# Stores of copied sums on ScalarE's queue, value copies on VectorE, fewer and larger transfers, and a guard between two finishing chunks

## The chip, the cores and the metric

The kernel runs on one core of a Trainium2 chip. The metric is device time in microseconds (us) of one execution; a kernel's time is the median of several runs. Engines are named as the profile names them: PE is TensorE (PEld its weight loads), DVE is VectorE, ACT is ScalarE, POOL is GpSimd and SP is SyncE. SPq, ACTq and so on are the instruction sequencers of these engines, where transfers (DMAs) are issued and where an engine waits for others. L1270 is line 1270 of the kernel before.

## The reference, cut to what matters

The input is x, 4 images of 128 channels and 64 x 64 positions, in float32. Layer 0 is a group norm, a deformable 3 x 3 convolution (offsets and masks from two small convolutions, four-corner bilinear samples) and a residual. Layer 1 takes the 4096 positions of an image as tokens and does attention with 16 heads of 8 values, a small feed-forward part, and a mixture of 8 experts, two per token:

```
x = x + deform_conv(group_norm(x))
t = to_tokens(x)
heads = layer_norm(t).reshape(B, S, 16, 8)
q = quantum_ring(heads + rx_theta)          # cosines and their running products
ctx = softmax(q @ q.T / sqrt(8)) @ q        # queries, keys and values are all q
x1 = layer_norm(ln_t + ctx @ w_comb.T + b_comb)
h = relu((cos(x1[:8]) * cos(ry)) @ w1.T + b1)
t = t + layer_norm(x1 + h @ w2.T + b2)
t = t + top2_experts(layer_norm(t))
```

Queries, keys and values are the same array q. The exponentials of the scores are most of the work: 4 images x 16 heads x 4096 x 4096, less what the symmetry of q @ q.T saves.

## The kernel before, in words

An image ("batch" b, 0 to 3) is cut into 8 chunks of 512 tokens (ch, or sc for a chunk of queries) and the 16 heads into 4 groups (g) of 4.

The main loop (from L1417) goes over **runs**. A run is one group and one chunk of queries against a list of key tiles t of 128 keys. For each key tile, one **step**, `scores` does 4 score matmuls on PE (L1261) and two exponentials of 128 x 1024 on ACT (L1270), and `context` sums with 4 matmuls on PE into one PSUM bank `acc` (L1281). A step takes two exponentials of 1.08 us each by their issue on ACT, some 1.86 us. Because the score matrix is symmetric, some runs give their exponentials transposed to another run (`turn`, L1140, on DVE, through DRAM), which multiplies them in `from_turned` (L1214).

Batch 0 has no earlier batch to hide its preparation behind. Its first runs use the chunks as they come, so their sums are partial. The first 26 runs (`run < opening`, `by_act` in the code) copy `acc` to an SBUF tile `cu` on ACT (L1491). `park_sums` has SP store `cu` to a DRAM tile `partd` (L1126), and the next run on the same group and chunk loads it back (L1456) and PE adds it into `acc` with the identity as weights. There are two `cu` tiles. From run 26 on DVE does the copies (L1493, L1495), and their stores stay on SP.

**Preparation** (`prepare`) of a batch is a generator. `deform` gathers corners from a DRAM table on POOL (L625), weighs and sums them on DVE (L645, L650, L651), transposes and parks them through DRAM (`smd`, L698 and L731). `convolved` does the convolution on PE for a chunk and ends in `features`: layer norm, cosines and products on DVE (to L822), then

* POOL copies the products q8 into the value tile `fx`, spaced by the column of ones (L823), and SP stores it to `fqd` in 4 transfers, one for each group (L827);
* PE transposes q8, DVE makes a high and a low part `hiT` and `loT` (L838, L839), and SP stores each twice into the keys `kTd` and twice into the queries `qTd` (L846, L847): 8 transfers of 256 KB.

`load_keys` and `load_queries` fetch them on SP (L1239, L1241, L1249).

**Finishing** (`finish`) of a chunk comes after the fourth group's context is parked: loads, `attention_out`, then `feed_forward` and `experts`, and a store of the result (L1081). Up to two finishing generators are alive at once, each taking the next chunk from the list `done`.

The order of all of this on PE, DVE, SP and POOL is written by a planner, the class `Beside`, while the program is built. In each step (`step`) it adds preparation, finishing and multiplications of turned exponentials beside the attention. A piece with PE work ("fill" below) is taken at most once a step after run 12, from a credit of 0.44 us a step, by rank: turned work first, finishing with ranks 1 and 2, preparation with 0.5 or 2. Work that must wait for something is put into a list by its planned time (`later`) and emitted when that time has come (`flush`). The planner only plans: on the chip every engine takes its own queue in order. After the last attention step, `drain` emits what is left, one job after the other. The exponentials on ACT are not ordered by hand.

The functions that the diff touches:

Of the kernel before, what the change touches and what calls it, by code (L numbers as in the profile page):

```python
# [22 lines left out]
P = 128  # L23
# [5 lines left out]
CH = 512  # L29
# [3 lines left out]
HD = 8  # L33
NGRP = 4
# [20 lines left out]
QG = 4 * QW  # L55
QL = QG
# [146 lines left out]
def need(pe=0.0, dve=0.0, lat=0.0, hold=False, after=0.0):  # L203

    return pe, dve, lat, hold, after


def ve(n, ops=1):  # L210

    return ops * (0.17 + n / 960.0)
# [6 lines left out]
def tr(n):  # L219

    return 0.13 + 0.115 * n
# [3 lines left out]
def kernel(  # L225
# [22 lines left out]
    nc = tc.nc  # L248
# [12 lines left out]
    beside = Beside()  # L261
# [11 lines left out]
    def misc(name):  # L273
        if alone:
            return ps_s.tile([P, 2, 512], F32, tag="sc", name=name)[:, 0, :]
        return ps_m.tile([P, 512], F32, tag="misc", name=name)
# [141 lines left out]
    for i in range(NFX):  # L418
        t = big.tile([P, 4, QR], F32, name=f"fx{i}")
        nc.gpsimd.memset(t, 0.0)  # L420
        h = t[:, :, : HEADS * QW].rearrange("p j (h d) -> p j h d", d=QW)
# [3 lines left out]
    def parked(shape, name, n=2):  # L425
        return [
            [dram.tile(shape, F32, name=f"{name}{i}_{c}") for c in range(NCH)] for i in range(n)
        ]

    x2d = parked([P, 4, C], "x2d", NB)  # L430
    fqd = parked([NGRP, P, 4, QL], "fqd")
    kTd = parked([P * NGRP, CH], "kTd")
    qTd = parked([P * NGRP, CH], "qTd")
# [3 lines left out]
    partd = [[dram.tile([P, CH], F32, name=f"part{g}_{c}") for c in range(NCH)] for g in range(NGRP)]  # L437
# [355 lines left out]
    def features(b, ch, x2, mean, rstd):  # L793

        yield from layer_norm_stats(x2, mean, rstd, "lt")

        def temp(name, shape=(P, 4 * C), dt=F32):
            return work.tile(list(shape), dt, tag="p2", name=f"{name}{b}_{ch}", bufs=NP2)

        fx, f4 = fxs[ch % NFX]  # L800
        xt, a, n, r = temp("xt"), temp("ra"), temp("rn"), temp("rr")
        yield need(dve=ve(128, 4))
        normalized(xt.rearrange("p (i c) -> p i c", c=C), x2, mean, rstd)
        beside.later(
            beside.dve,
            lambda: nc.sync.dma_start(out=xtd[b][ch].rearrange("p i c -> p (i c)"), in_=xt),
        )
        yield need(dve=ve(512, 2))
        a8 = a.rearrange("p (h d) -> p h d", d=HD)
        x8 = xt.rearrange("p (h d) -> p h d", d=HD)  # L810
        nc.vector.tensor_tensor(a8, x8, rx_sb[:, None, :].to_broadcast([P, 64, HD]), ALU.add)
        yield from cosine(a, a, n, r, ve(512))
        c8 = a.rearrange("p (j h d) -> p j h d", j=4, d=HD)
        q8 = n.rearrange("p (j h d) -> p j h d", j=4, d=HD)
        yield need(dve=ve(64, 7))
        nc.vector.tensor_tensor(q8[:, :, :, 0], c8[:, :, :, 1], c8[:, :, :, 2], ALU.mult)
        for d in range(3, HD):
            nc.vector.tensor_tensor(q8[:, :, :, 0], q8[:, :, :, 0], c8[:, :, :, d], ALU.mult)
        yield need(dve=ve(64, 7), lat=0.2)
        nc.vector.tensor_tensor(q8[:, :, :, 1], c8[:, :, :, 0], c8[:, :, :, 1], ALU.mult)  # L820
        for d in range(2, HD):
            nc.vector.tensor_tensor(q8[:, :, :, d], q8[:, :, :, d - 1], c8[:, :, :, d], ALU.mult)  # L822
        beside.later(beside.dve, lambda: nc.gpsimd.tensor_copy(f4[:, :, :, :HD], q8))  # L823

        def put_values():
            for g in range(NGRP):
                nc.sync.dma_start(out=fqd[b % 2][ch][g], in_=fx[:, :, QG * g : QG * g + QL])  # L827

        beside.later(beside.dve + 2.0, put_values)

        yield need(pe=tr(4), dve=ve(512, 2))
        pt = misc(f"fT_ps{b}_{ch}")
        for i in range(4):
            nc.tensor.transpose(pt[:, P * i : P * (i + 1)], n[:, P * i : P * (i + 1)], ident)
        hi, lo = temp("hiT"), temp("loT")
        nc.vector.tensor_copy(hi.bitcast(F32R), pt)  # L838
        nc.vector.tensor_tensor(lo.bitcast(F32R), pt, hi, ALU.subtract)  # L839

        def put(part, fT):

            kd = kTd[b % 2][ch].rearrange("(h l r d) n -> l r h d n", l=2, r=2, d=HD)
            qd = qTd[b % 2][ch].rearrange("(h r l d) n -> l r h d n", l=2, r=2, d=HD)
            for rep in range(2):
                nc.sync.dma_start(out=kd[part, rep], in_=fT)  # L846
                nc.sync.dma_start(out=qd[part, rep], in_=fT)  # L847

        beside.later(beside.dve - ve(512), lambda: put(0, hi))
        beside.later(beside.dve, lambda: put(1, lo))  # L850
        prepared[b, ch] = beside.dve + 9.0
        featuring.pop(0)

# [41 lines left out]
    def attention_out(b, ch, r, aT, a4):  # L895


        yield need(dve=ve(512))
        nc.vector.tensor_tensor(r, r, bc4(b_comb), ALU.add)
        yield need(dve=ve(512), lat=0.2)  # L900
        nc.vector.tensor_tensor(aT, aT, a4.rearrange("p i c -> p (i c)"), ALU.mult)
        for i in range(4):
            if i % 2 == 0:
                yield need(pe=2 * MM128, dve=ve(512) if i else 0.0, lat=0.0 if i else FREE, hold=not i)
            if i == 0:
                po = misc(f"ao_ps{b}_{ch}")
            by_columns(
                po[:, C * i : C * (i + 1)], aT[:, P * i : P * (i + 1)], wcomb_sb, True, True
            )
        nc.vector.tensor_tensor(r, r, po.rearrange("p (i c) -> p i c", c=C), ALU.add)  # L910
        m = work.tile([P, 4], F32, tag="ln_m", name=f"m1{b}_{ch}")
        rs = work.tile([P, 4], F32, tag="ln_r", name=f"r1{b}_{ch}")
        yield from layer_norm_stats(r, m, rs, "ln")
        yield need(dve=ve(128, 4))
        normalized(a4, r, m, rs)
        yield need(dve=ve(512, 2), lat=0.2)
        nc.vector.tensor_tensor(a4, a4, bc4(g1), ALU.mult)
        nc.vector.tensor_tensor(a4, a4, bc4(beta1), ALU.add)
# [165 lines left out]
    def finish(b, ch):  # L1084
        x4 = temp2(f"x4_{b}_{ch}")
        nc.sync.dma_start(out=x4, in_=x2d[b][ch])

        rows = atd[b][ch].rearrange("g (h d) n -> (g h) d n", d=32)
        aT = temp2(f"aT{b}_{ch}", (P, CH))
        nc.sync.dma_start(out=aT, in_=rows[:, :HD])  # L1090
        rd = work.tile([P, CH // HD], F32, tag="rd", name=f"rd{b}_{ch}")
        nc.sync.dma_start(out=rd, in_=rows[:, HD].rearrange("h (q n) -> h q n", q=HD))
        r = temp2(f"r{b}_{ch}")
        nc.sync.dma_start(out=r, in_=xtd[b][ch])
        yield need(lat=4.0)
        yield need(dve=0.6, lat=0.1)
        nc.vector.reciprocal(rd, rd)
        yield need(lat=3.5)
        nc.sync.dma_start(out=rdd[b][ch].rearrange("h q n -> (h q) n"), in_=rd)
        yield need(lat=6.0)  # L1100
        a4 = temp2(f"a4_{b}_{ch}")
        nc.sync.dma_start(
            out=a4.rearrange("p i c -> p (i c)"),
            in_=rdd[b][ch].rearrange("h q n -> h (q n)")[:, None, :].to_broadcast([HEADS, HD, CH]),
        )
        yield from attention_out(b, ch, r, aT, a4)
        yield from feed_forward(b, ch, x4, a4)
        yield from experts(b, ch, x4)


    def park_context(b, g, sc, cu):
# [8 lines left out]

        beside.later(beside.dve, put)

    def park_sums(g, sc, cu, when):

        def put():
            nc.sync.dma_start(out=partd[g][sc], in_=cu)  # L1126
            storing.discard((g, sc))

        storing.add((g, sc))
        beside.later(when, put)  # L1130

# [90 lines left out]

    landing = {}
    fetched = {}
    groups, done, active = {}, [], []

    def finishing():

# [125 lines left out]
    for n, (run, t) in enumerate(steps):  # L1356
        b, g, sc = runs[run][:3]
# [50 lines left out]
    n = issued = begun = 0  # L1408
    beside.rate = 1.0
    with tc.manual_schedule(engines={PE, DVE, SP, POOL}):  # L1410
# [6 lines left out]
        while n < len(steps):  # L1417
# [10 lines left out]
            run, t = steps[n]  # L1428
            b, g, sc, ts, kind = runs[run]
# [21 lines left out]
            if t == ts[0]:  # L1451
                if kind in (MORE, LAST):
                    if (g, sc) in storing:
                        beside.flush()
                    cu = work.tile([P, 512], F32, tag="cu", name=f"cu{run}", bufs=NCU)
# [23 lines left out]
            by_act = run < opening  # L1479
# [8 lines left out]
            if kind in (WHOLE, FIRST):  # L1488
                cu = work.tile([P, 512], F32, tag="cu", name=f"cu{run}", bufs=NCU)
            if by_act:  # L1490
                nc.scalar.copy(cu, acc)  # L1491
            elif kind in (WHOLE, FIRST):
                nc.vector.tensor_copy(cu, acc)  # L1493
            else:
                nc.vector.tensor_tensor(cu, cu, acc, ALU.add)  # L1495
            if kind in (WHOLE, LAST):
                park_context(b, g, sc, cu)
            else:
                park_sums(g, sc, cu, beside.now + 3.0 if by_act else beside.dve)
        alone.append(True)  # L1500
        beside.drain()

# [72 lines left out]
```

## Time and profile before

| | us |
|---|---|
| median of 11 runs | 7601.65 |
| lowest and highest | 7593.96 and 7617.57 |
| the profiled execution | 7605.18 |
| span of its profile, from the first to the last instruction | 7603.2 |

| engine | busy us | share of the span |
|---|---|---|
| PE | 7126.1 | 94% |
| ACT | 6865.0 | 90% |
| DVE | 4465.9 | 59% |
| PEld | 2378.2 | 31% |
| POOL | 1661.8 | 22% |

The DMA engines moved 1689.51 MB in 909788 packets. Busy shares are means over stages with different limits: the first 900 us, in which batch 0 is prepared, and the last 83 us, in which nothing but finishing is left, look different from the middle. The idle time in front of an instruction is put down to what released it.

### The profile page before, as it was taken

The numbers are of one execution on the slowest core, as the hardware profiler recorded it, in microseconds if no ns is written. First come the engines' busy times: TensorE is split into PE (matmuls) and PEld (weight loads), VectorE is DVE, ScalarE is ACT, GpSimd is POOL, SyncE is SP. The second block draws the span as 40 slices with busy tenths as digits, with TensorE's granted clock in tenths as the row PEclk, the third lists the DMA queues.
The fourth block names the chain that finished last, engine by engine and source line by source line (L and its number), as shares of the span: only waits on it lengthen the run. The fifth ranks groups of instructions, "written<-read, shape, count | busy, mean of one in ns | idle before, by whom it ended". The sixth has DMA issues, their size and how long they took to land.

```text
span 7603.2 us, 180754 instructions
## 1 busy us (share of the span) xinstructions
PE 7126.1 (94%) x73848; PEld 2378.2 (31%) x73848; DVE 4465.9 (59%) x8950; ACT 6865.0 (90%) x7467; POOL 1661.8 (22%) x1326
## 2 busy tenths in 40 slices
PE   3689999899999999999999999989999999999997
PEld 2122222223333333333333323323333333333333
DVE  6756356667444867776554677766444544555534
ACT  0578999889999999999999988989999999999995
POOL 5544034443000432422000334431000000000000
PEclk6799999999999999999999999999999999999998
DMA  5677567978445878887645688897454466666661
GB/s 178 210 214 222 139 220 239 296 230 294 149 170 196 294 232 270 279 279 240 210 177 183 232 280 296 284 316 248 174 182 161 142 232 232 233 221 243 222 204 64
DMA packets 909788, 1689.51 MB, mean 222 GB/s; under 512 B 150754, under 2 KB 384124, under 8 KB 858268
## 3 DMA queue, kind: packets, MB, share of 16 engines
q1 hardware_dynamic: 809102, 1371.37, 54.4%
q0 software_dynamic: 92160, 302.06, 12.1%
q8 instruction: 579, 9.49, 0.5%
q10 hardware_dynamic: 7694, 4.52, 0.2%
q14 instruction: 253, 2.07, 0.1%
HBM read 1027.51 MB, written 650.14 MB: 221 GB/s over the span
## 4 chain that ended last, share of the span: by engine, by line
PE 83%; DMA 7%; DVE 4%; issue 2%; ACT 2%; SPq 1%; POOL 1%; another core or an unknown queue 1%; ACTq 0%; POOLq 0%; DVEq 0%
PE acc L1281 40%; PE sc L1261 25%; PE acc L1214 5%; PE e_ps L281 4%; PE conv_ps L281 4%; DMA et<-etd 3%; PE f_ps L281 2%; ACT e L1270 2%; DMA sT<-smd 1%; PE om_ps L533 1%; DVE v L645 1%; DMA etd<-st 1%; POOL v L625 1%; DMA cu<-part 0%
## 5 line engine op out<-in xcount | busy, mean ns | idle before, releaser
L1270 ACT ACTIVATE e<-sc 128x1024 f32<-128x1024 f32 x7400 | 6850.7, 1079 | 553.3 <-PE sc L1261 369.7
L1281 PE MATMUL acc<-e,qf 128*9 128x512 f32 (+1 forms) x29600 | 3942.5, 601 | 28.1 <-ACT cu L1491 10.4
L1261 PE MATMUL sc<-qT,kT 32*128 32x512 f32 x14800 | 2373.4, 499 | 167.1 <-ACT e L1270 92.6
L1261 PEld LDWEIGHTS sc<-qT,kT 32*128 32x128 f32 x14800 | 945.1, 183 | 3629.5 <-ACT e L1270 3109.1
L625 POOL DMA_INDIRECT v<-tab,idx x1152 | 1458.8, 1266 | 1589.4 <-DVE tr L686 961.7
L1140 DVE STREAM_TRANSPOSE st<-e 128x1024 f32<-128x1024 f32 x792 | 937.3, 1222 | 763.3 <-ACT e L1270 663.0
L1281 PEld LDWEIGHTS acc<-e,qf 128*9 128x9 f32 (+1 forms) x29600 | 682.5, 91 | 623.9 <-issue 352.1
L396 POOL TENSOR_TENSOR r<-ln_t,expo 128x4 f32<-128x4 f32 x96 | 112.2, 1169 | 3107.2 <-DVE ln_t L394 3059.9
L645 DVE TENSOR_TENSOR v<-v,wt 128x1536 f32<-128x1536 f32 x384 | 667.0, 1737 | 113.5 <-DMA v<-tab,idx 88.7
L1214 PE MATMUL acc<-et,qv 128*9 128x128 f32 x12672 | 508.9, 277 | 59.1 <-DMA et<-etd 49.0
L1065 DVE TENSOR_TENSOR eo<-e_ps,gt 128x512 f32<-128x512 f32 x256 | 175.2, 686 | 557.1 <-PE e_ps L281 550.5
L650 DVE TENSOR_TENSOR v<-v 128x768 f32<-128x768 f32 x384 | 367.2, 956 | 10.1
L281 PE MATMUL conv_ps<-sT,wconv_sb 128*32 128x256 f32 x4320 | 350.5, 398 | 9.3 <-DMA sT<-smd 7.0
L1214 PEld LDWEIGHTS acc<-et,qv 128*9 128x9 f32 x12672 | 270.2, 90 | 262.8 <-issue 216.1
L686 DVE STREAM_TRANSPOSE tr<-v 128x128 f32<-128x128 f32 x1080 | 249.5, 282 | 38.2 <-DMA etd<-st 29.3
L1493 DVE COPY cu<-acc 128x512 f32<-128x512 f32 x116 | 80.2, 692 | 303.0 <-PE acc L1281 255.3
L651 DVE TENSOR_TENSOR v<-v 128x384 f32<-128x384 f32 x384 | 215.8, 562 | 13.3
L396 POOL TENSOR_TENSOR rstd<-lt_t,expo 128x4 f32<-128x4 f32 x32 | 59.4, 1855 | 581.1 <-DVE lt_t L394 557.6
L281 PE MATMUL f_ps<-w_sb,h 128*32 128x128 f32 x4096 | 165.6, 281 | 0.0
L950 DVE TENSOR_SCALAR h<-h_ps,b_sb 128x512 f32<-128x512 f32 x128 | 94.9, 744 | 100.2 <-PE h_ps L948 94.3
L758 DVE SCALAR_TENSOR_TENSOR xr<-conv_ps,bconv_sb,xr 128x128 f32<-128x128 f32 x128 | 35.9, 344 | 191.2 <-PE conv_ps L281 170.8
L823 POOL COPY fx<-rn 128x512 f32<-128x512 f32 x32 | 26.9, 840 | 527.3 <-DVE rn L822 319.1
(227 smaller groups left out, 3153.5 us busy)
## 6 DMA issues: line engine op xcount, KB each, us to landing
etd<-st SPq DMA_DIRECT2D x396, 1024.0 KB
et<-etd SPq DMA_DIRECT2D x396, 1024.0 KB
kT<-kTd SPq DMA_DIRECT2D x372, 256.0 KB
smd<-tr SPq DMA_DIRECT2D x360, 192.0 KB
sT<-smd SPq DMA_DIRECT2D x360, 192.0 KB
qT<-qTd SPq DMA_DIRECT2D x166, 256.0 KB
atd<-cu SPq DMA_DIRECT2D x128, 256.0 KB
qf<-fqd SPq DMA_DIRECT2D x372, 72.0 KB
```

Source lines behind the costliest of these rows:

```text
L281: nc.tensor.matmul(dst[c : c + 32], lhsT=lhsT[:, c : c + 32], rhs=rhs, start=start, stop=stop)
L625: nc.gpsimd.indirect_dma_start(out=v[:, k, :], out_offset=None, in_=tab, in_offset=bass.IndirectOffsetOnAxis(ap=idx[:, j, kk : kk + 1], ax ...
L645: nc.vector.tensor_tensor(v4, v4, w12[:, :, None].to_broadcast([P, 12, C]), ALU.mult)
L650: nc.vector.tensor_tensor(v[:, :, : 2 * C], v[:, :, : 2 * C], v[:, :, 2 * C :], ALU.add)
L651: nc.vector.tensor_tensor(v[:, :, :C], v[:, :, :C], v[:, :, C : 2 * C], ALU.add)
L686: nc.vector.transpose(out=tr9[:, k, :, j % 4, :], in_=v[:, k, :C].rearrange("p (c i) -> p c i", i=32),)
L1065: nc.vector.tensor_tensor(ws[hf], pe.rearrange("p (e c) -> p e c", c=C), gt[:, i, 4 * hf : 4 * (hf + 1), None].to_broadcast([P, 4, C]), AL ...
L1140: nc.vector.transpose(out=st[:, :, 2 * pr : 2 * pr + 2, :].rearrange("p o h (q j) -> p o (h q) j", j=32), in_=es[pr].rearrange("p h (q o i ...
L1214: nc.tensor.matmul(acc[32 * h : 32 * h + QW, P * kt : P * (kt + 1)], lhsT=qv[:, at : at + QW], rhs=e[:, :, h, 32 * t : 32 * (t + 1)], star ...
L1261: nc.tensor.matmul(ps[i // 2][:, i % 2, :], lhsT=kT[h : h + 32, P * (t % 4) : P * (t % 4 + 1)], rhs=qT[h : h + 32, :], start=True, stop=True,)
L1270: nc.scalar.activation(e, ps[pr], AF.Exp, scale=1.0 / math.sqrt(HD))
L1281: nc.tensor.matmul(acc[32 * h : 32 * h + width, :], lhsT=flat[:, first : first + width], rhs=es[h // 2][:, h % 2, :], start=(t == ts[0]), ...
```

## The change

Four things are changed.

1. In the first 26 runs the store of `cu` to `partd` is issued by ScalarE, right behind its copy, and not by SyncE. `park_sums` keeps the later runs, and such a store no longer stands in `storing` (whose members make L1454 emit all deferred work before a reload).
2. The products q8 are copied to the value tile by VectorE, behind the low part of the transposed features, and not by GpSimd.
3. A chunk's keys, queries and values go to DRAM in 5 transfers, not 12: each of the two parts once to the keys and once to the queries, both copies by one transfer that reads its source twice, and the values of all groups in one. For this the 32 rows of a head are in another order in DRAM, the same for keys and queries. The values now come last.
4. In `finish`, a list `heavy` lets only one finishing chunk at a time be in `feed_forward` and `experts`; the other waits ahead of them.

```diff
         for d in range(2, HD):
             nc.vector.tensor_tensor(q8[:, :, :, d], q8[:, :, :, d - 1], c8[:, :, :, d], ALU.mult)
-        beside.later(beside.dve, lambda: nc.gpsimd.tensor_copy(f4[:, :, :, :HD], q8))
-
-        def put_values():
-            for g in range(NGRP):
-                nc.sync.dma_start(out=fqd[b % 2][ch][g], in_=fx[:, :, QG * g : QG * g + QL])
-
-        beside.later(beside.dve + 2.0, put_values)
-
-        yield need(pe=tr(4), dve=ve(512, 2))
+        yield need(pe=tr(4), dve=ve(512, 3))
         pt = misc(f"fT_ps{b}_{ch}")
...
         nc.vector.tensor_tensor(lo.bitcast(F32R), pt, hi, ALU.subtract)
+        nc.vector.tensor_copy(f4[:, :, :, :HD], q8)
 
         def put(part, fT):
-            kd = kTd[b % 2][ch].rearrange("(h l r d) n -> l r h d n", l=2, r=2, d=HD)
-            qd = qTd[b % 2][ch].rearrange("(h r l d) n -> l r h d n", l=2, r=2, d=HD)
-            for rep in range(2):
-                nc.sync.dma_start(out=kd[part, rep], in_=fT)
-                nc.sync.dma_start(out=qd[part, rep], in_=fT)
-
-        beside.later(beside.dve - ve(512), lambda: put(0, hi))
-        beside.later(beside.dve, lambda: put(1, lo))
+            kd = kTd[b % 2][ch].rearrange("(p l r) n -> l p r n", l=2, r=2)
+            qd = qTd[b % 2][ch].rearrange("(p r l) n -> l p r n", l=2, r=2)
+            twice = fT[:, None, :].to_broadcast([P, 2, CH])
+            nc.sync.dma_start(out=kd[part], in_=twice)
+            nc.sync.dma_start(out=qd[part], in_=twice)
+
+        def put_values():
+            nc.sync.dma_start(
+                out=fqd[b % 2][ch].rearrange("g p t x -> p t g x"),
+                in_=fx.rearrange("p t (g x) -> p t g x", g=NGRP),
+            )
+
+        beside.later(beside.dve - 2.0 * ve(512), lambda: put(0, hi))
+        beside.later(beside.dve - ve(512), lambda: put(1, lo))
+        beside.later(beside.dve, put_values)
         prepared[b, ch] = beside.dve + 9.0
...
         yield from attention_out(b, ch, r, aT, a4)
+        while heavy:
+            yield need(lat=1.0)
+        heavy.append(True)
         yield from feed_forward(b, ch, x4, a4)
         yield from experts(b, ch, x4)
+        heavy.pop()
...
-    def park_sums(g, sc, cu, when):
+    def park_sums(g, sc, cu):
...
-        beside.later(when, put)
+        beside.later(beside.dve, put)
...
             if by_act:
                 nc.scalar.copy(cu, acc)
+                nc.scalar.dma_start(out=partd[g][sc], in_=cu)
             elif kind in (WHOLE, FIRST):
...
-            else:
-                park_sums(g, sc, cu, beside.now + 3.0 if by_act else beside.dve)
+            elif not by_act:
+                park_sums(g, sc, cu)
```

More of the change, by code (lines that the diff above doesn't have):

```diff
@@ L1226 @@
     fetched = {}
-    groups, done, active = {}, [], []
+    groups, done, active, heavy = {}, [], [], []
     def finishing():
```

## The prediction

> **What bounds the kernel now.** I read the slices of the page first, then the busy time by stage, then who waited for whom on the queue that issues the transfers (SPq), then the timeline of the finishing work.
>
> ```profile
> PE   3689999899999999999999999989999999999997
> ...
> ACT  0578999889999999999999988989999999999995
> ```
>
> ```profile
> 188.00:650.00 462.00, 355.48 (x2790) 100.52 (x2786) 298.77 (x549) 315.44 (x350) 245.52 (x184) 0.84 0.72 221
> ...
> 5300.00:7517.00 2217.00, 2214.20 (x24984) 767.13 (x24984) 1056.01 (x2452) 2214.76 (x2421) 53.29 (x52) 1.00 0.58 200
> 7517.00:7603.20 86.20, 36.32 (x461) 21.56 (x457) 53.73 (x149) 2.36 (x4) 3.02 (x3) 0.66 0.07 23
> ```
>
> The first two lines are the 40 slices, in tenths. The window lines give the stretch and its length, then busy PE, PEld, DVE, ACT and POOL, the clock, the DMA share and GB/s. From 5300 to 7517 us ACT is busy 2214.8 of 2217 us: the exponentials (L1270, 1.08 us each) are the bound, and nothing beside them can shorten this part. Three places are not bound by them. From 188 to 650 us, where the first 26 runs lie, ACT idles 462.0 - 315.4 = 146.6 us: batch 0's chunks come every 100 us or so (the products at L822 end at 154, 255, 350, 468, 577, 685, 787 and 871 us), and attention waits for them. Between 905 and 5300 us ACT loses some 300 us in pieces beside the preparation. And from 7517 us only finishing is left: 86 us, ACT busy 2.4.
>
> ```profile
> SPq L1126 <- ACT cu L1491: 122.1, 16, 23.9
> ...
> SPq L1126 <- DMA cu<-part: 18.4, 6, 5.5
> ```
>
> These are SyncE's waits from 180 to 660 us (total, times, longest): 122.1 + 18.4 us in front of the stores of the copied sums, with the queue behind them held up.
>
> ```profile
> 7253.52 0.42 SPq L1086 DMA_DIRECT2D x<-x2d  x1
> ...
> 7260.14 0.34 SPq L1081 DMA_DIRECT2D out_dram<-y_3T  x1
> ...
> 7262.35 0.38 SPq L1081 DMA_DIRECT2D out_dram<-y_4T  x1
> ...
> 7316.45 0.42 SPq L1086 DMA_DIRECT2D x<-x2d  x1
> ...
> 7461.08 0.35 SPq L1081 DMA_DIRECT2D out_dram<-y_5T  x1
> ...
> 7521.37 1.03 SPq L1086 DMA_DIRECT2D x<-x2d  x1
> ...
> 7531.88 0.35 SPq L1081 DMA_DIRECT2D out_dram<-y_6T  x1
> ...
> 7599.64 0.34 SPq L1081 DMA_DIRECT2D out_dram<-y_7T  x1
> ```
>
> This is the end of the timeline of SyncE: L1086 begins a chunk's finishing, L1081 stores its result. Chunks 3 and 4 of the last batch come out together, 5 and 6 overlap, and chunk 6 is still at its last expert matmuls when attention ends at 7520 us. Finishing runs behind attention for most of the kernel (batch 3's chunk 5 has its last group parked, L1114, at 7110 us and its load only at 7254) and catches up only here. So its pace sets the tail.
>
> **The change, part by part.**
>
> *The guard (`heavy`).* It removes no instruction. It takes away the overlap of two chunks between the z transposes (L939) and the y transposes (L890), where 36 of a chunk's 38 fills lie. What one chunk needs there nearly alone is in the timeline of PE:
>
> ```profile
> 6079.14 0.61 PE L939 MATMUL z_ps<-ident,zx 128*32 128x128 f32 x4
> ...
> 6226.58 0.66 PE L890 MATMUL y_ps<-ident,x 128*128 128x128 f32 x4
> ...
> 6494.51 0.61 PE L939 MATMUL z_ps<-ident,zx 128*32 128x128 f32 x4
> ...
> 6640.04 0.66 PE L890 MATMUL y_ps<-ident,x 128*128 128x128 f32 x4
> ...
> 7299.09 0.61 PE L939 MATMUL z_ps<-ident,zx 128*32 128x128 f32 x4
> ...
> 7459.67 0.66 PE L890 MATMUL y_ps<-ident,x 128*128 128x128 f32 x4
> ```
>
> That is 147, 146 and 161 us. I counted the fills of the other chunk in these stretches from the trace: 6, 4 and 13. Taking a step of 1.86 us off for each gives 136 to 138 us, a lower end, since they also fill steps in which this chunk waits for its own layer norm or softmax. Some 3 us lie ahead of the first z transpose (L927 to L939 of one chunk). So with the guard a chunk takes 139 to 164 us; I take 149, by the two stretches with the least of the other in them.
>
> Two overlapping chunks do better. From the z transposes at 5217 us (preparation ends at 5311) to the end of attention at 7520, 17 chunks come out, and chunk 6 has 12 of some 53 us left: 17.8 chunks in 2303 us, 130 us each. With the guard it is 2303 / 149 = 15.5, so 2.3 chunks more are left when attention ends; at 139 us 1.2, at 164 us 3.7. Nothing covers them there. Alone, a chunk takes from L927 (7546.4) to its store (7599.6) 53 us, so the tail grows by 2.3 x 53 = 122 us (64 to 196). If one chunk alone were as fast as the pair, it would cost nothing, or give back up to 8 us: chunk 7's reciprocal stores only at 7532.3, right behind chunk 6's last work, though its load went out at 7521.4. I take +115, a little under the middle, because an earlier end of the one chunk frees fills for the next.
>
> *The stores on ScalarE.* Removed from SP: 26 issues of 0.32 us (L1126) and the waits before them, 140.5 us. They do not all count. Where the stuck store has loads behind it that are due, the chain of batch 0 gets longer: SP stands at 291.9 to 299.6 us with the last `sT<-smd` loads of a convolution behind it (7.7 us), at 380.3 to 385.6 with a chunk's `smd` stores (5.3), and at 517, 532 and 610 us for 5 to 6 us each. The chain of waits has 3.7% of its first 1000 us, 37 us, in `DMA cu<-part`, PE waiting for sums whose reload was issued late. Some 4 to 5 us for each of four or five chunks: -20 us. The bounds are 0, if the convolution's fills, one a step, set the pace anyway, and -45, the 37 us and the first 7.7. ScalarE pays 26 issues of 0.32 (L1126) to 0.44 us (its own loads, L296): 8 to 11 us, and it must wait out its own copy of 0.59 us, with the next exponentials queued behind; 11 + 26 x 0.59 = 26 us at most. The 146.6 us of idle ACT hide it; without them it would be these 26. The gain reaches the end only if chunk 7's keys also come earlier, for ACT waits 11.7 us for them at 905 us; they end the same chain.
>
> The Trainium skill says ("DMA: Bandwidth & Descriptors", Issuing engines are not separate DMA queues) that transfers started by different engines end up on the same DMA engines, so that another issuer saves only its sequencer's time. By that rule alone the part is worth the 26 x 0.32 = 8 us of issue and not 20; the waits of the queue above speak for the larger number.
>
> *The copy on VectorE.* POOL loses 32 copies (L823, median 0.61 us on `fx`), and the gathers behind them start up to 0.8 us earlier (468.00 to 468.79 us in one chunk). DVE gains 32 copies of 512 elements: 0.43 us by L373, 0.69 by L838, the PSUM copy; on DVE 14 to 22 us over the kernel, 7 x 0.43 to 7 x 0.69 = 3 to 5 us in the chain to chunk 7, against at most 7 x 0.8 = 6 us gained there. DVE idles 15 to 24 us a chunk at L758, and later it is at 48% (1056 of 2217 us). I take 0, between -6 and +5.
>
> *Five transfers for twelve.* The bytes stay. SP issues 4 x 0.63 (L827) + 8 x 0.65 (L846, L847) = 7.7 us a chunk now. Four larger ones cost the same 0.65 or up to twice that, the values 0.63 to 4 x 0.63: 3.2 to 7.7 us. The saving, 0 to 4.5 us a chunk, lies ahead of the key loads; it counts in the first four chunks, 0 to -18 us. The values now land last, but the score matmuls and exponentials come before their first use. I take -5, near the low end, since the loads wait for the bytes too. In the middle of the kernel SP waits for DVE far more (L1149, 1309 us in all) and I take 0, with +-15 us for another order of the plan.
>
> The sum: 7605.2 + 115 - 20 - 5 = 7695 against the profiled execution; its time is 3.5 us over the median of 7601.65, so 7692.
>
> **The rivals.**
>
> *Faster: the guard is free.* Finishing could be limited by the credit (0.44 us a step) and the single spare PSUM bank, so that the second chunk only takes what the first would have had. For it: turned work takes its fills first, either way. Against it: 147 and 146 us nearly alone, 130 each in pairs. It decides below 130 us a chunk. Then 7601.65 - 25 = 7577, with the 8 us of the tail 7569.
>
> *The cancel:* the guard costs some 20 us (about 134 us a chunk) and the opening gives it back: 7600.
>
> *ScalarE becomes late:* its stores hold exponentials back in the opening by 26 us, the SP waits come back at the reloads, and the guard costs its 115: 7740.
>
> *It doesn't do what it says:* the order of deferred work could shift so that two chunks rarely meet at the guard. That is the first rival's time.
>
> **How the numbers follow.** The guard at its price: 0.61, 7692, own range 7635 to 7750. Guard free or nearly: 0.26, 7565 to 7586. Cancel: 0.07. Late ScalarE: 0.06, 7740. Within 0.2% (15 us, about what this kernel's measurement can tell from no change) lies the cancel, so faster 0.26, same 0.07, slower 0.67. The range runs from 7570 to 7750: it leaves out some 0.07 below (a larger gain in the opening) and some 0.1 above (a guard at 164 us a chunk).
>
> **What would show it.** In the profile after: one chunk at a time between L939 and L890 (new lines), results every 140 to 160 us after 5300 us, two or three stores of results after the last exponential block, and the stretch from there to the end at some 190 us, not 83. In the opening: no SP wait for the ACT copies, products of the chunks some 20 us earlier by chunk 4, ACT idle in 188 to 650 us down from 147. Results every 130 us or less with the guard, or a tail of 75 to 85 us, would prove the first step wrong; unchanged times of the chunks' products, the second.

## The result and the profile after

The changed kernel takes 7912.13 us (median of 8 runs, 7897.21 to 7921.29), the kernel before 7602.4 us beside it: a ratio of 1.0405, 95% interval 1.0395 to 1.0414. The forecast was 7692, slower, with a range up to 7750. The direction was right; the loss is 310 us where 90 were forecast. The profiled execution of the changed kernel has a span of 7920.1 us, and all that follows compares it with the span of 7603.2 before.

In the slices of the page, nearly all of PE's and ACT's row is as it was, and the last two digits are not:

```profile
PE   3679999999999999999999899999999999999954
...
ACT  0679999899999888899999888899999999999910
```

The windows by stage (busy PE, PEld, DVE, ACT, POOL, then the granted clock as a share of TensorE's full clock, the DMA share and GB/s) show which stages grew:

```profile
188.00:650.00 462.00, 343.59 (x2782) 98.62 (x2778) 298.90 (x551) 313.99 (x349) 238.36 (x180) 0.85 0.74 221
5300.00:7561.00 2261.00, 2256.40 (x24745) 770.67 (x24744) 1001.89 (x2241) 2258.87 (x2469) 45.41 (x46) 1.00 0.58 202
7561.00:7920.10 359.10, 147.62 (x1755) 87.04 (x1754) 220.33 (x656) 1.37 (x6) 14.98 (x15) 0.61 0.06 18
```

From 5300 us to its end, attention is bound by ACT as before (2258.9 of 2261 us). The stretch without attention is now 359 us and not 84. ACT's idle time in the opening, 462.0 - 314.0 = 148 us, is what it was (147).

The instructions of the exponentials' line (count, shortest, median and longest ns, first and last start) give the end of attention, before and after:

```profile
L1270 ACT ACTIVATE e<-sc x7400: 1005/1058/1519, 177.6 to 7518.0; 128x1024 f32<-128x1024 f32 x195
```

```profile
L1275 ACT ACTIVATE e<-sc x7400: 1015/1070/1499, 179.9 to 7559.7; 128x1024 f32<-128x1024 f32 x195
```

So the 317 us of the two spans are 42 us by which attention ends later (7519.1 to 7560.8, with the last exponential's own time) and 275 us of a longer tail (84.1 to 359.3). The end of SyncE's timeline shows what the tail is made of (L1087 begins a chunk's finishing, L1082 stores its result):

```profile
7502.85 0.35 SPq L1082 DMA_DIRECT2D out_dram<-y_1T  x1
...
7581.00 0.33 SPq L1087 DMA_DIRECT2D x<-x2d  x1
...
7588.29 0.34 SPq L1082 DMA_DIRECT2D out_dram<-y_2T  x1
...
7656.44 0.34 SPq L1082 DMA_DIRECT2D out_dram<-y_4T  x1
...
7724.66 0.34 SPq L1082 DMA_DIRECT2D out_dram<-y_5T  x1
...
7792.87 0.34 SPq L1082 DMA_DIRECT2D out_dram<-y_6T  x1
...
7861.17 0.34 SPq L1082 DMA_DIRECT2D out_dram<-y_7T  x1
...
7916.67 0.34 SPq L1082 DMA_DIRECT2D out_dram<-y_3T  x1
```

When attention ends at 7561, chunk 2 is 27 us from its store and five more are wholly or mostly undone: 4, 5, 6 and 7 at 68.2 us each, then chunk 3, which had waited at the guard and needs 55.5. That is 27.4 + 4 x 68.2 + 55.5 + 3.4 = 359 us. Before, one chunk and a quarter were left.

The guard's pace beside attention is in PE's timeline (z transposes L940, y transposes L891), and so is its pace with nothing beside it:

```profile
7206.83 0.61 PE L940 MATMUL z_ps<-ident,zx 128*32 128x128 f32 x4
...
7350.64 0.66 PE L891 MATMUL y_ps<-ident,x 128*128 128x128 f32 x4
...
7361.64 0.61 PE L940 MATMUL z_ps<-ident,zx 128*32 128x128 f32 x4
...
7606.89 1.01 PE L940 MATMUL z_ps<-ident,zx 128*32 128x128 f32 x4 [10.43 <-DVE zx L936]
...
7650.73 0.44 PE L891 MATMUL y_ps<-ident,x 128*128 128x128 f32 x2
...
7674.99 1.01 PE L940 MATMUL z_ps<-ident,zx 128*32 128x128 f32 x4 [10.43 <-DVE zx L936]
```

This chunk takes 143.8 us from z to y, and 11.0 more pass until the next one's z: 154.8. That is the slow end: from the z transposes at 5465 us to those at 7509 the 14 chunks take 120 to 155 us each, 146 on average. In the tail it is 43.8 and 24.3: 68.1. The same four transposes take 1.01 us there and 0.61 beside attention; the granted clock is 0.61 in the tail and 1.00 ahead of it.

The waits of SyncE's queue from 180 to 660 us no longer name the ACT copies, but they name others:

```profile
SPq L1254 <- PE sc L1266: 45.1, 7, 12.2
SPq L840 <- DVE hiT L831: 41.6, 3, 17.4
SPq L698 <- DVE tr L686: 32.8, 7, 13.1
...
SPq L1461 <- DMA part<-cu: 27.2, 3, 11.8
```

Over all rows of that view the queue waited 272 us before and 316 us after. The reload (L1461) now waits for the store that ScalarE issued.

### The profile page after: what moved, and what is told of

Its sections match the earlier page's. It is cut to its first block, busy times and chain, and to the rows that moved or that the text cites. A ratio compares the mean times of both kernels' runs of the same rounds, so it can differ in the third digit from the quotient of the medians.

```text
span 7920.1 us, 180370 instructions
## 1 busy us (share of the span) xinstructions
PE 7234.7 (91%) x73848; PEld 2425.8 (31%) x73848; DVE 4487.4 (57%) x8982; ACT 6858.8 (87%) x7467; POOL 1619.9 (20%) x1294
## 4 chain that ended last, share of the span: by engine, by line
PE 80%; DMA 7%; DVE 5%; issue 3%; ACT 2%; SPq 1%; POOL 1%; another core or an unknown queue 0%; ACTq 0%; POOLq 0%; DVEq 0%
PE acc L1286 38%; PE sc L1266 24%; PE acc L1219 5%; PE conv_ps L281 4%; PE e_ps L281 3%; DMA et<-etd 2%; PE f_ps L281 2%; ACT e L1275 2%; DMA sT<-smd 1%; PE om_ps L533 1%; DMA cu<-part 1%; DMA etd<-st 1%; DVE v L645 1%; POOL v L625 1%; PE ao_ps L281 1%
## 5 line engine op out<-in xcount | busy, mean ns | idle before, releaser
L1266 PE MATMUL sc<-qT,kT 32*128 32x512 f32 x14800 | 2433.3, 499 | 174.4 <-ACT e L1275 94.7
L1266 PEld LDWEIGHTS sc<-qT,kT 32*128 32x128 f32 x14800 | 974.3, 183 | 3668.5 <-ACT e L1275 3193.3
```

The costliest lines, as they stand in the source:

```text
L1266: nc.tensor.matmul(ps[i // 2][:, i % 2, :], lhsT=kT[h : h + 32, P * (t % 4) : P * (t % 4 + 1)], rhs=qT[h : h + 32, :], start=True, stop=True,)
```

## The experiments

The runs were made on other chips as well, where the kernel before took 7461.5 us (first four runs), 7460.2 (next four) and 7578.3 (last four); so ratios to the kernel before on the same chip are compared, and times only within a group.

The theory (G) was that the guard alone makes the loss, the other parts being small. The rival (M) was that the other three parts, each of them entered in the planner's costs, move the plan and make a good share of it.

**The guard alone** (the kernel before with it):

```diff
         yield from attention_out(b, ch, r, aT, a4)
+        while heavy:
+            yield need(lat=1.0)
+        heavy.append(True)
         yield from feed_forward(b, ch, x4, a4)
         yield from experts(b, ch, x4)
+        heavy.pop()
...
-    groups, done, active = {}, [], []
+    groups, done, active, heavy = {}, [], [], []
```

> The kernel before with the guard of the change alone (one finishing chunk at a time in feed_forward and experts); the stores, copies and transfers stay as before. Theory G (the guard sets the tail): results every 150 to 158 us, 4 to 6 chunks left when the last exponential of attention ends, each some 68 us, so 250 to 350 us behind attention and a time of 7850 to 7950 us. Theory M (the other three parts put back finishing by another order of the plan): the tail stays under 120 us, time under 7660. For the 42 us by which attention itself ends later after the change: if the guard does that too, attention ends at 7550 to 7590 us here; if the new transfers or copies do it, at 7515 to 7530.

Measured: 7788.51 us, ratio 1.0440 (1.0425 to 1.0455), more than the whole change. Attention ends at 7441.2 us, 71 us later than in the run with the stores alone (7370.2, which took the time of the kernel before), and the tail is 339.0.

**The change without the guard** (with 13 instead of 11 buffers for the finishing tiles, `NF2`; without the guard it was not tried with 11):

```diff
-NF2 = 11
+NF2 = 13
...
-        while heavy:
-            yield need(lat=1.0)
-        heavy.append(True)
...
-        heavy.pop()
```

> The change without its guard: stores on ScalarE, copies on VectorE, 5 transfers, two chunks at once in feed_forward and experts, and 13 buffers of the finishing tiles (tag f2) instead of 11, so that two chunks have room. Theory G: tail back to 75 to 95 us; with the opening's gain of 17 us and no loss in the middle the time is 7575 to 7600. Theory M: the tail stays over 200 us, 7800 to 7900. If the loss in the middle (attention's end) comes from the transfers or copies, attention ends at 7550 to 7570 us and the time is 7630 to 7660.

Measured: 1.0018 (1.0008 to 1.0029), tail 78.3 us, one result after the end of attention. G stands: the guard is the loss, though 1.0018 is a little over the time that G gave (0.997 to 1.000 of before), since the gain of the opening that it counted on isn't there.

**The stores on ScalarE alone:**

```diff
                 nc.scalar.copy(cu, acc)
+                nc.scalar.dma_start(out=partd[g][sc], in_=cu)
...
-            else:
-                park_sums(g, sc, cu, beside.now + 3.0 if by_act else beside.dve)
+            elif not by_act:
+                park_sums(g, sc, cu, beside.dve)
```

> The kernel before with the stores of the first 26 runs issued by ScalarE alone. The opening's theory (SyncE's waits before these stores hold up the convolution's loads): 5 to 20 us faster, 7580 to 7597, no wait of SyncE for the ACT copies, products of chunk 4 earlier by 5 to 20 us. Rival (the convolution's matmuls, one fill a step, set the pace anyway): 7595 to 7605.

Measured: 0.9999 (0.9991 to 1.0008). Nothing. In the opening, too: chunk 7's products end at 851.0 us, and at 846.7 in the kernel with 13 buffers and the stores on SyncE (below, on a chip where the kernel before takes the same time within 2 us). SyncE's waits from 180 to 660 us sum to 322 and 315 us in these two.

**Five transfers alone** (the key, query and value transfers of the change; POOL keeps the copy):

```diff
...
-            for rep in range(2):
-                nc.sync.dma_start(out=kd[part, rep], in_=fT)
-                nc.sync.dma_start(out=qd[part, rep], in_=fT)
+            twice = fT[:, None, :].to_broadcast([P, 2, CH])
+            nc.sync.dma_start(out=kd[part], in_=twice)
+            nc.sync.dma_start(out=qd[part], in_=twice)
```

> The kernel before with keys, queries and values in 5 transfers a chunk instead of 12 and the new order of the 32 rows of a head in DRAM; copy on GpSimd, stores on SyncE, no guard. By the prediction's term: 0 to 18 us faster in the first four chunks, 7585 to 7602. If the larger transfers are what delays attention in batches 2 and 3: 7625 to 7665, with the loss between 2300 and 5300 us.

Measured: 0.9985 (0.9977 to 0.9994), 11 us less.

The guard's 327 us were still nearly three times the forecast's +115, and 71 of them lay in attention, where the forecast had nothing. The next runs split them. **The guard late** (shown against the guard alone; `n` counts the attention's steps; with 13 buffers, as in the next run):

```diff
-        while heavy:
+        while heavy and 2500 <= n < len(steps):
```

> The kernel before with the guard alone, and that only from step 2500 on (about 5160 us, the end of the preparations) to the last step of the attention; 13 instead of 11 buffers for the finishing tiles, since two chunks may be in both parts at the switch. With the guard all along the time was 1.044 of before. Theory 'both halves': no chunk and no attention is lost ahead of 5200 us (14 results by 5300 us, attention ending at 7365 to 7395 us), then 154 us a chunk over 2200 us give 14.3 chunks instead of 17, 2.7 more left at the end at 62 us each: a tail of 240 to 260 us, ratio 1.020 to 1.025. Theory 'pace at the end only' (the step of the prediction, only mis-sized): this half carries nearly the whole loss, five results after the last exponential, ratio 1.035 to 1.044.

Measured: 7578.39 against 7460.16 us, +118 us, ratio 1.0159 (1.0143 to 1.0174). Attention ends at 7365.9, the tail is 208.2 us. "Both halves" had the sign of each part and missed the tail's size (240 to 260) and the ratio (1.020 to 1.025); "pace at the end only" is refuted.

**The guard early:**

```diff
-        while heavy:
+        while heavy and n < 2500:
```

> The kernel before with the guard alone, and that only up to step 2500 (about 5160 us), 13 instead of 11 buffers for the finishing tiles. Theory 'both halves': the guard costs attention 60 to 75 us beside the preparation of batches 2 and 3 and leaves two chunks more to do at 5300 us (12 results, not 14), which the pairs at 130 us each can't catch up: attention ends at 7430 to 7450 us, a tail of 180 to 210 us, ratio 1.022 to 1.027. Theory 'pace at the end only': the chunks that were held back are caught up after 5300 us and attention loses under 20 us: ratio under 1.008.

Measured: 7612.47 us, +152 us, ratio 1.0201 (1.0185 to 1.0216). Attention ends at 7468.8 us, 96 us later than with 13 buffers alone (7373.1, below), and the tail is 155.4, 72 us longer than its 83.5. (The two add up to 168 us and not 152, since the profiled execution is 14 us above the median.) The guard had been gone for 2200 us by then. So the larger half arises beside the preparations, about half of it or more in attention; "both halves" had said less there (7430 to 7450) and more in the tail (180 to 210). By 5300 us this run had stored 11 results, that with 13 buffers alone 13; one of these two chunks was caught up by the pairs, the other was not. With the guard all along nothing can be caught up: 118 + 152 = 270 us, and the remaining 57 of the 327 would be about one chunk of the tail (68); that is argued from the sizes and was not tried.

**The guard, and a drain by the planner's steps:**

```diff
         alone.append(True)
+        beside.fills = 8
+        for _ in range(600):
+            if not beside.queue and not beside.deferred:
+                break
+            beside.step(1.5)
         beside.drain()
```

> The kernel before with the guard alone, as in the first run of this study (1.044), but the work left after the last attention step is put out by the planner's steps and not one job after the other, so that the loads and the attention output of the next chunk can lie beside the experts of the one ahead. Attention must end as in that run (7441 us). If the 68 us that each left chunk takes are 44 us of its own chain (z transposes to y transposes) and 24 us of loads and attention output that only the order of the drain keeps out of the overlap, five chunks save 24 each: a tail of 210 to 240 us, ratio 1.026 to 1.031. If the 68 us are bound by PE, DVE or the DMAs of the chunk itself, the tail stays at 330 to 340 us and the ratio at 1.043 to 1.045.

Measured: 1.0374 (1.0358 to 1.0390), tail 298.2 us. The stores in SyncE's timeline:

```profile
7571.18 0.34 SPq L1081 DMA_DIRECT2D out_dram<-y_4T  x1
...
7630.16 0.34 SPq L1081 DMA_DIRECT2D out_dram<-y_5T  x1
...
7687.31 0.34 SPq L1081 DMA_DIRECT2D out_dram<-y_6T  x1
```

59 and 57 us a chunk and not 68, nor the 44 that I expected. PE's timeline of this run shows where the time went:

```profile
7508.23 0.44 PE L890 MATMUL y_ps<-ident,x 128*128 128x128 f32 x2
...
7517.70 1.01 PE L939 MATMUL z_ps<-ident,zx 128*32 128x128 f32 x4 [4.53 <-DVE zx L935]
...
7565.48 0.44 PE L890 MATMUL y_ps<-ident,x 128*128 128x128 f32 x2
```

From y to the next z it is 9.5 us here and not 24.3, so the order of the drain made some 15 of the 24; what is left is as long as beside attention (7 to 11). But from z to y a chunk now takes 48 to 50 us and not 44, which gives some 5 of the 15 back.

**Thirteen buffers alone** (`NF2 = 13` in the kernel before, the control for the runs above that have 13):

> The kernel before with 13 instead of 11 buffers for the finishing tiles and nothing else. The run without the guard had 13 and took 1.0018 of before, though the stores on ScalarE alone gave 0.9999 and the five transfers alone 0.9985. If the buffers are the cause (a second chunk begins earlier and takes fills from turned work or preparation): 1.002 to 1.004. If the copy on VectorE or the joint plan is: 0.999 to 1.001.

Measured: 0.9998 (0.9989 to 1.0007). The buffers cost nothing.

**The guard, with the preparations held back.** Why should a guard between two finishing chunks delay attention? PE's waits from 2400 to 5300 us give a lead (total, times, longest): first the stores alone, which stand for the kernel before on that chip, then the guard alone.

```profile
PE acc L1214 <- DMA et<-etd: 42.3, 15, 8.2
...
PE conv_ps L281 <- DMA sT<-smd: 4.8, 2, 3.0
```

```profile
PE acc L1218 <- DMA et<-etd: 67.6, 18, 9.6
PE conv_ps L281 <- DMA sT<-smd: 34.2, 7, 12.9
```

The first row is turned exponentials that haven't landed, the second convolutions of the preparation that stand on PE ahead of their inputs. With the guard, the second grows from 4.8 to 34.2 us. One such wait in PE's timeline of the guard alone; the scores that feed ACT are behind it:

```profile
2982.28 0.51 PE L1265 MATMUL sc<-qT,kT 32*128 32x512 f32 x4
2995.67 1.08 PE L281 MATMUL conv_ps<-sT,wconv_sb 128*32 128x256 f32 x8 [12.88 <-DMA sT<-smd]
2996.49 1.97 PE L1285 MATMUL acc<-e,qf 128*9 128x512 f32 x8
2998.39 0.80 PE L1265 MATMUL sc<-qT,kT 32*128 32x512 f32 x4
```

And the preparation of batch 2 ran ahead: the stores of its last keys begin at 3463 us, not 3586. So a third theory: the fills that the guard denies the second chunk go to preparation. The test gives each convolution the attention step at which the kernel before planned it:

```diff
+        pace = {2: (1115, 1187, 1267, 1350, 1415, 1476, 1561, 1647), 3: (2033, 2091, 2151, 2211, 2270, 2327, 2389, 2444)}
+        while b in pace and n < pace[b][ch]:
+            yield need(lat=1.0)
         xr = work.tile([P, CH], F32, tag="p2", name=f"xr{b}_{ch}", bufs=NP2)
```

> The kernel before with the guard alone (1.044 in the first run of this study) and one thing more: each chunk's convolution in the preparations of batches 2 and 3 may not begin before the attention step at which the kernel before planned it. With the guard the preparation of batch 2 ran some 125 us ahead, and attention lost 71 us between 2800 and 5200 us. Theory 'freed fills': the fills that the guard keeps from the second chunk go to preparation, whose convolutions then stand on PE ahead of their inputs and stop the scores; held back, attention ends at 7370 to 7395 us, the tail stays at 330 to 350 us, ratio 1.034 to 1.038. Theory 'late turned work' (attention loses its time at the loads of turned exponentials and at other waits, whatever preparation does): attention ends at 7430 us or later and the ratio is 1.043 or more.

Measured: 1.0314 (1.0297 to 1.0330). Attention ends at 7474.2 us, where the kernel before, with 7578 us on this chip and a tail of 84, would end it at some 7494. The loss in attention is gone. The windows from 2400 to 5300 us show it without that estimate (the fourth number of busy time is ACT's): the guard alone and the stores alone, which ran on one chip, then this run and that with the stores and the five transfers (below), which ran on another.

```profile
2400.00:5300.00 2900.00, 2754.43 (x29002) 914.13 (x28998) 1879.72 (x3574) 2701.08 (x2934) 773.73 (x621) 0.98 0.76 251
```

```profile
2400.00:5300.00 2900.00, 2811.93 (x30424) 942.89 (x30420) 1968.41 (x3854) 2773.14 (x3015) 793.32 (x630) 0.99 0.77 257
```

```profile
2400.00:5300.00 2900.00, 2802.89 (x29438) 930.96 (x29434) 1884.77 (x3555) 2735.41 (x2968) 794.57 (x627) 0.99 0.77 253
```

```profile
2400.00:5300.00 2900.00, 2801.39 (x29830) 938.59 (x29826) 1963.98 (x3798) 2728.20 (x2958) 799.98 (x634) 0.99 0.77 255
```

The guard takes 72 us of ACT's busy time, and with the preparations held back nothing is missing. Both of PE's waits are under those of the first fence of waits:

```profile
PE acc L1221 <- DMA et<-etd: 29.7, 7, 8.3
...
PE conv_ps L281 <- DMA sT<-smd: 0.6, 1, 0.6
```

(On this run's own chip the kernel with the stores and the five transfers has 17.2 and 1.9 us there.) The tail is not gone: 360.8 us, with 11 results by 5300 us. "Freed fills" holds for attention, though the ratio came out a little under its 1.034: attention ends some 20 us ahead of the estimate for the kernel before, and the profiled execution is even 16 us above its median. Where this gain comes from was not tried. Nor do the two waits make the whole loss: with the guard alone they grew by 29 us (convolutions) and 25 us (turned exponentials), 54 of 71.

**The stores and the five transfers together,** without guard and VectorE copy:

> The kernel before with the stores of copied sums on ScalarE and the five transfers for twelve, without the guard and without the copy on VectorE. Alone they gave 0.9999 and 0.9985. If both are independent: 0.998 to 0.999, so a little faster than both kernels. If the plan's order decides and not the parts: anywhere from 0.998 to 1.002.

Measured: 7561.18 against 7578.27 us, ratio 0.9975 (0.9965 to 0.9984). This is faster than both kernels. Its interval overlaps that of the five transfers alone, so whether the stores add anything here is open.

**The same with the drain by steps** (the diff of the guard's run with it):

> The kernel of the run with stores and five transfers, and the work after the last attention step put out by the planner's steps as in the run that tried this with the guard. There it took 50 us off five left chunks. Here only chunk 7 and the end of chunk 6 are left, a tail of some 84 us: if the overlap of chunk 7's loads and attention output with chunk 6's experts counts, 8 to 15 us less than without it, ratio 0.997 to 0.998. If the tail is one chunk's own chain: the same as without, within 0.1%.

Measured: 0.9976 (0.9966 to 0.9985), tail 83.5 us against 83.4 without. With one chunk left there is nothing to overlap.

**The copy on VectorE alone** (13 buffers):

```diff
-        beside.later(beside.dve, lambda: nc.gpsimd.tensor_copy(f4[:, :, :, :HD], q8))
...
-        beside.later(beside.dve + 2.0, put_values)
...
-        yield need(pe=tr(4), dve=ve(512, 2))
+        yield need(pe=tr(4), dve=ve(512, 3))
...
+        nc.vector.tensor_copy(f4[:, :, :, :HD], q8)
...
-        beside.later(beside.dve - ve(512), lambda: put(0, hi))
-        beside.later(beside.dve, lambda: put(1, lo))
+        beside.later(beside.dve - 2.0 * ve(512), lambda: put(0, hi))
+        beside.later(beside.dve - ve(512), lambda: put(1, lo))
+        beside.later(beside.dve, put_values)
```

So the value stores also move behind those of keys and queries.

> The kernel before with the value copy on VectorE alone and 13 buffers for the finishing tiles (which by themselves gave 0.9998). The change without its guard took 1.0018, though two of its other parts gave 0.9999 and 0.9985. If the copy is the difference, here 1.002 to 1.004, by VectorE's 32 copies in the planned backlog; if it costs what its duration says, 14 to 22 us spread beside other work: 0.9995 to 1.0005.

Measured: 1.0084 (1.0070 to 1.0099), 64 us, more than either reading allowed. The copies themselves are as cheap as they were costed; this is their group in the profile of the changed kernel (busy us, mean ns, idle before):

```profile
L833 DVE COPY fx<-rn 128x512 f32<-128x512 f32 x32 | 13.5, 423 | 0.0
```

The 64 us are all in attention, which ends at 7559.2 us, against some 7494 by the estimate above and 7479.7 with the stores and the five transfers; the tail is 78.3. The line of the low parts `loT` shows the preparations' ends, here and then in the run with the stores and the five transfers:

```profile
L836 DVE TENSOR_TENSOR loT<-fT_ps,hiT x32: 691/691/692, 156.7 to 5640.8; 128x512 fp32r<-128x512 f32 x32
```

```profile
L841 DVE TENSOR_TENSOR loT<-fT_ps,hiT x32: 691/692/693, 157.5 to 5265.9; 128x512 fp32r<-128x512 f32 x32
```

Batch 3 is prepared 375 us later, and PE waits 54.9 us for turned exponentials from 2400 to 5300 us, against 17.2. It is a shift of the plan, like that under the guard but in the other direction. The late preparation alone is not the price: in the change without the guard batch 3 is ready at 5474.8 us, 318 later than with the stores alone (5156.8), and that run took 1.0018. Which of the planner's decisions flips, and whether for 0.7 us of planned VectorE work a chunk or for the new place of the value stores, is not shown.

## Why the prediction was right in direction and wrong in size

**The guard: the mechanism was right, the stretch was too short.** The term of +115 us was worked out for the time from 5217 us on, and there it holds: the guard from step 2500 on (about 5160 us) costs 118 us. That is in part luck: its two factors were each off and made up for each other. "2.3 chunks more" are 125 us of tail / 68.2 = 1.8 in that run, and "53 us" each are 68.2. The 53 were read from L927 of chunk 7 on; in a row of left chunks the loads and the attention output ahead of L927 count as well, and the drain puts them out one chunk after the other. The pace, 149 us, was nearly right: 146 on average in the changed kernel, with which the forecast's own sum leaves 17.8 - 2303 / 146 = 2.0 chunks. Its parts were off here too: from one y to the next z are 7 to 11 us and not 3, and from z to y often less than the 146 and 147 that I took.

**The step that failed is what it left out: the time ahead of 5217 us.** The sum took the chunks done by then, and the end of attention, from the kernel before. By 5300 us there are 11 results, not 13, because the guard has been at work since the first finished chunk at some 1980 us (the first `zf`, L933, is at 1981). These two chunks at 68.2 us are 136 us. With 1.8 x 68.2 = 123 they make 259 of the 275 us by which the tail grew. The forecast had noted that "finishing runs behind attention for most of the kernel", and drew no price from it.

**A second thing left out: who gets the freed fills.** "An earlier end of the one chunk frees fills for the next" was the only use that I saw. They went to the preparation of batch 2, and PE then stood longer before convolutions without inputs (34.2 us, not 4.8) and before turned exponentials: 71 us of attention for the guard alone, none with the preparation held to its old steps. In the whole change attention lost 42. The windows before and after show a loss like that of the guard alone, 69 us of ACT's busy time from 2400 to 5300 us, and 20 us gained from 900 to 2400:

```profile
900.00:2400.00 1500.00, 1427.07 (x13629) 450.60 (x13629) 848.22 (x1565) 1380.79 (x1496) 399.06 (x324) 0.98 0.70 224
2400.00:5300.00 2900.00, 2789.80 (x29564) 930.70 (x29563) 1950.81 (x3763) 2708.55 (x2936) 797.60 (x632) 0.99 0.76 253
```

```profile
900.00:2400.00 1500.00, 1441.40 (x13779) 456.34 (x13783) 850.17 (x1545) 1400.58 (x1517) 396.62 (x315) 0.98 0.70 226
2400.00:5300.00 2900.00, 2741.77 (x28347) 904.52 (x28347) 1855.84 (x3510) 2639.88 (x2864) 763.54 (x612) 0.98 0.75 246
```

But PE's waits for convolution inputs grow there only from 2.5 to 6.7 us, and those for turned exponentials from 28.7 to 54.6. So the mechanism is shown for the guard alone; how much of the 69 us it makes in the whole change stays open.

**The stores on ScalarE: -20 us forecast, nothing measured** (interval -7 to +6 us). The queue's waits were taken as time of batch 0's chain. In the whole change the products of chunks 1 to 5 end 9, 7, 8, 5 and -1 us earlier, and chunk 7's at 866.9 instead of 870.6; with the stores alone chunk 7's are not earlier at all (851.0 us, and 846.7 in the kernel with 13 buffers). ACT's idle time stayed at 148 us. The place was empty, and others moved in: the waits of the queue summed to 316 us, not 272, in the whole change, and with the stores alone to 322, not 315. The forecast had weighed two sizes. The 20 us came from the rows of the queue's waits. The other, an estimate of 8 us, came by the rule of the Trainium skill ("DMA: Bandwidth & Descriptors", Issuing engines are not separate DMA queues) that another issuer saves only its sequencer's time. The runs allow a gain of no more than 7 us, so the smaller size was the nearer one.

**Five transfers: -5 forecast, -11 measured alone.** In the changed kernel the medians of the five issues are 0.37, 0.54, 0.77, 1.24 and 1.30 us: 4.2 a chunk, within the 3.2 to 7.7 given.

**The copy on VectorE: 0 forecast, +64 alone.** Its duration was right and its place in the plan was not costed. Beside the other parts this price isn't seen: the guard alone has 1.0440, the whole change 1.0405, and the stores with the five transfers would account for 0.0025 of the 0.0035 between them, if the ratios add. Without the guard it may be the 0.004 by which 1.0018 stands above 0.9975.

**The rivals.** "The guard is free" needed under 130 us a chunk; 146 on average rule it out. "The cancel" would have needed a guard of 20 us and the opening to give back what it didn't. "ScalarE becomes late" was right in one part, SP waiting at the reloads (27.2 us); the 26 us of late exponentials don't show (the stores alone took -7 to +6 us), and its 7740 was nearly as far off as the forecast. Of the signs named ahead, one chunk at a time came true, and so did results every 140 to 160 us but for two of 118 and 119; "two or three stores after the last exponentials, some 190 us" were six and 359.

## What to carry to other kernels

A constraint on background work acts for the whole time that the work runs. Price its backlog from the first piece on, then what each left piece costs with nothing beside it, and not only the stretch next to the end.

A slot that is taken from one background job is given to another. Ask which one, and whether that one then stands at the head of an in-order queue without its inputs. Where a planner works from hand-set costs, a small edit (here 0.7 us a chunk and another place for a store) can cost far more than its duration: 64 us here.

Time that a queue waits is not time of the chain. Where the queue has other things to wait for, a removed wait is replaced by the next.

## What the runs showed of the hardware

A left chunk pays twice for being alone: nothing hides its waits, and the granted clock in the tail is 0.61 against 1.00 beside attention, where the same four transposes take 0.61 us and not 1.01. PE is busy only 147.6 of the tail's 359.1 us; how much of the 68.2 us a chunk the clock makes was not measured by itself.

A transfer that reads its source twice (512 KB) took 0.37 to 1.24 us to issue, by the medians of line and part, 0.73 on average; one of 256 KB took 0.65 before. With the same bytes, five issues a chunk took 4.2 us and twelve 7.7: 0.84 us each and 0.64. So the price went more with the number of issues than with the bytes.
